# First layer of the edges' net made transposed in four column groups of PE, and one sum moved to GpSimd

## The chip, the cores and the metric

The kernel runs on one core of one Trainium2 chip. The core has engines that each take their own instructions in order: PE (TensorE, matrix products; PEld is its loading of the held operand), DVE (VectorE), ACT (ScalarE), POOL (GpSimd, which here also issues the gathers) and SP (SyncE, which issues plain transfers). The metric is the device time of one execution, in microseconds (us). Before the change it is 2907.54 us, the median of three runs (2907.07 to 2909.65).

## The reference

The layer works on 3125 nodes of 512 values and 50000 edges between them, sorted by the node they end in. It adds a message-passing part and a linear attention to the nodes, then a mixture of eight experts. What the change touches is the message of an edge:

```python
ip1 = jnp.einsum('eum,eum->eu', p1[edge_dst], p1[edge_src]) / 3.0
s0 = jnp.concatenate([pd0, pd0, ip1], axis=-1)
w = ssp(edge_attr @ W_f1) @ W_f2 * (ssp(s0 @ W_s1) @ W_s2)
w1, w2, w3, w4 = jnp.split(w, 4, axis=-1)
out0 = w1 * x0e * sh0[:, None] + w4 * (jnp.einsum('eum,em->eu', x1e, sh1) / jnp.sqrt(3.0))
out1 = w2[:, :, None] * x0e[:, :, None] * sh1[:, None, :] + w3[:, :, None] * x1e * sh0[:, None, None]
out = jax.ops.segment_sum(edge_feat, edge_dst, num_segments=old_x.shape[0])
```

Here `s0` has three blocks of 128 per edge. The first two are values of the end node, so their share of `s0 @ W_s1` (32 values) is made once per node; only `ip1 @ W_s1[256:]` is left for each edge. `x1e . sh1` is a sum of three terms, one for each component.

## The kernel before, in words

All is fp32. A first stage lays the edges out in records sorted by end node, scatters them with GpSimd, makes the nodes' values, and writes two tables of rows to memory: `rows_d` (416 values for the end node, the first 32 of them its share of the first layer) and `rows_s` (896 for the start node). The second stage is the loop over the edges. The third stage runs the experts.

The loop works on tiles of 128 edges, two tiles to a pair (a step `s`), two pairs to a quad `q`. There are 212 pairs always run and some more under a condition on the chip, which does not hold here. The order of PE, ACT, DVE and POOL in it is the order of the code in `run_pairs`, written out by hand: each step runs pieces of several quads and pairs, and `due(n)` says for which quad a piece is due `n` pairs ahead of the pair that is being summed up. The pieces that matter here:

- `fetch` (nine pairs ahead): POOL issues four gathers a step, two of `gd` rows (L710) and two of `gx` rows (L714); SP loads the quad's records `rec` (L699). `gd` has three buffers of a quad, so a new one waits for its last reader three quads before.
- `products` (L726, DVE), `turn` (L734, PE, twelve transposes that also sum the three components of `ip1`) and `turn2` (L743, ACT): `ip`, with features on the partitions.
- `hidden` (four pairs ahead): PE multiplies `ip`, held, with `w_s1c` (L750), for each tile 128 edges by 32; ACT copies the other net's first layer `h1` out of the records (L752).
- `hidden2` (three ahead): DVE adds the end node's share from `gd` (L758). `softplus` on ACT (L763, L766, L769) and `softplus2` on DVE (L774, two ahead) make the shifted softplus.
- `turn_hidden`: PE transposes both first layers, 128 edges by 4 tiles x 32, so that the 32 hidden values of tile `i` lie on partitions 32i to 32i+31 (L779, L780); ACT copies them to `hT` (L785).
- `weigh` (one ahead): PE multiplies 32-row slices of `hT` with the second layers, for two tiles of each net (L801, L805), ACT scales and copies the first (L808, L811), DVE multiplies with the second (L812).
- `dots` (L822, ACT, two ahead) makes the first two terms of `x1 . sh1`; `dots2` (one ahead, DVE) adds them (L830) and adds the third term (L832).
- `which` (L842), `feats` (L860, L867 on ACT, L871, L876): the message. `gather_up` (L884) sums messages into their nodes on PE, `keep_sums` (L893) adds them to the nodes.
- In every sixth step POOL also issues a transfer of an expert's weights (L900).

The PSUM pool `ps_a` has one buffer of each name, `work` has two.

Of the kernel before, what the change touches and what calls it, by code (L numbers as in the profile page):

```python
# [8 lines left out]
F32 = mybir.dt.float32  # L9
I32 = mybir.dt.int32  # L10
AF = mybir.ActivationFunctionType
ALU = mybir.AluOpType
# [4 lines left out]
P = 128  # L17
# [3 lines left out]
G = 4  # L21
REC = 48
USED = 40
CT = 28
HID = 32
# [18 lines left out]
def gnn_mix_moe_kernel(ctx: ExitStack, tc: tile.TileContext, a: dict, out: bass.AP):  # L44
# [5 lines left out]
    nc = tc.nc  # L50
# [25 lines left out]
    ident = const.tile([P, P], F32, name="ident")  # L76
# [46 lines left out]
    with ExitStack() as c1:  # L123
# [313 lines left out]
        work = c1.enter_context(tc.tile_pool(name="work1", bufs=2, reuse_waits="tile"))  # L437
# [42 lines left out]
        for g in range(2):  # L480
            nc.scalar.copy(kx[:, g, :], ps_kx[g])
            ps = psum.tile([P, 4, P], F32, name="ps_kxT", tag="mm")
# [3 lines left out]
            ps = psum.tile([P, GH * HD], F32, name="ps_kv", tag="mm")  # L486
            for k in range(4):
                nc.tensor.matmul(
                    ps, kxT[:, k, g * P : (g + 1) * P], w_v[:, k, g * GH * HD : (g + 1) * GH * HD],
                    start=(k == 0), stop=(k == 3),  # L490
# [4 lines left out]
            ps = psum.tile([P, 2, P], F32, name="ps_kvT", tag="mm")  # L495
# [3 lines left out]
            ps = psum.tile([P, D], F32, name="ps_kvw", tag="mm")  # L499
# [4 lines left out]
            ps = psum.tile([P, 1], F32, name="ps_ks", tag="mm")  # L504
# [4 lines left out]
        for k, w_nd in enumerate((w_nd0, w_nd1)):  # L509
# [4 lines left out]
            ps = psum.tile([P, P], F32, name="ps_ww", tag="mm")  # L514
# [9 lines left out]
        for c in range(NCH):  # L524
            m = cn(c)
            cols = slice(c * CH, c * CH + m)
            for g in range(2):
                ps = psum.tile([P, CH], F32, name="ps_q", tag="mm")
# [5 lines left out]
                ps = psum_b.tile([P, CH], F32, name="ps_nm", tag="mb")  # L534
# [23 lines left out]
        for c in range(NCH):  # L558
            m = cn(c)
            cols = slice(c * CH, c * CH + m)  # L560
            hT = work.tile([P, 2, CH], F32, name="hT", tag="pair")
            for f in range(2):
                ps = psum.tile([P, CH], F32, name="ps_g1", tag="mm")
# [5 lines left out]
            for f in range(2):  # L569
                ps = psum.tile([P, CH], F32, name="ps_g2", tag="mm")  # L570
# [11 lines left out]
            ps = psum.tile([P, CH], F32, name="ps_p0", tag="mm")  # L582
# [3 lines left out]
            for t in tiles_of(c):  # L586
# [6 lines left out]
                ps = psum.tile([P, HID + 3 * MUL], F32, name="ps_p1", tag="mm")  # L593
                nc.tensor.matmul(ps[:n, :HID], p0[:, lo : lo + n], w_s1p, start=True, stop=True)
                for b in range(3):
                    nc.tensor.matmul(
                        ps[:n, HID + b * P : HID + (b + 1) * P], xT[:, 1 + b, t * P : t * P + n], w_pre1,
                        start=True, stop=True,
                    )
                nc.scalar.copy(r[:n, : HID + 3 * MUL], ps[:n])  # L600
                ps = psum.tile([P, D], F32, name="ps_nd", tag="mm")
                for b in range(4):
                    nc.tensor.matmul(
                        ps[:n, b * P : (b + 1) * P], xg[:, b, lo : lo + n], w_nd0 if b == 0 else w_nd1,
                        start=True, stop=True,
# [8 lines left out]
                ps = psum_b.tile([P, D], F32, name="ps_own", tag="mb")  # L614
# [4 lines left out]
                for b in range(4):  # L619
                    last = nc.tensor.matmul(  # L620
                        ps[:n, b * P : (b + 1) * P], xg[:, b, lo : lo + n], w_ndo[0 if b == 0 else 1],
                        start=False, stop=(b == 3),
# [43 lines left out]
    with ExitStack() as c2:  # L666
        w = c2.enter_context(tc.tile_pool(name="w2", bufs=1, reuse_waits="tile"))
        gat = c2.enter_context(tc.tile_pool(name="gat", bufs=4, reuse_waits="tile"))
        work = c2.enter_context(tc.tile_pool(name="work2", bufs=2, reuse_waits="tile"))
        ps_a = c2.enter_context(tc.tile_pool(name="ps_a", bufs=1, space=PSUM, reuse_waits="tile"))  # L670
# [3 lines left out]
        w_s1c = w.tile([P, HID], F32, name="w_s1c")  # L674
# [17 lines left out]
        quads = [Quad() for _ in range(NQ)]  # L692

        def fetch(q, k):

            Q = quads[q]
            if k == 0:
                Q.rec = gat.tile([P, G, REC], F32, name="rec2", bufs=6)
                loaded = nc.sync.dma_start(  # L699
                    Q.rec, recs[q * G * P : (q + 1) * G * P, :].rearrange("(p i) f -> p i f", i=G)  # L700
                )
# [3 lines left out]

                Q.gd = gat.tile([P, G, HID + 3 * MUL], F32, name="gd", bufs=3)
                Q.gx = gat.tile([P, G, 3 * MUL + D], F32, name="gx", bufs=5)
            reci = Q.rec.bitcast(I32)
            for i in (2 * k, 2 * k + 1):
# [33 lines left out]
            nc.scalar.copy(Q.ip, Q.ps_ip)  # L743

        def hidden(q):
            Q = quads[q]
            Q.ps = ps_a.tile([P, 3, P], F32, name="ps_h")
            ps = Q.ps[:, 2, :].rearrange("p (i f) -> p i f", f=HID)
            for i in range(G):
                nc.tensor.matmul(ps[:, i, :], Q.ip[:, i, :], w_s1c, start=True, stop=True)  # L750
            Q.h1 = work.tile([P, G, HID], F32, name="h1")
            nc.scalar.copy(Q.h1, Q.rec[:, :, 8:USED])  # L752

        def hidden2(q):
            Q = quads[q]
            Q.h = work.tile([P, G, HID], F32, name="h2")
            ps = Q.ps[:, 2, :].rearrange("p (i f) -> p i f", f=HID)
            nc.vector.tensor_add(Q.h, ps, Q.gd[:, :, :HID])  # L758

        def softplus(q):  # L760
            Q = quads[q]
            sp = work.tile([P, G, HID], F32, name="sp")
            nc.scalar.activation(sp, Q.h, AF.Abs)  # L763
            if q * PR < NPR_MOST:
                with tc.issue_after(table.ins):
                    nc.scalar.activation(sp, sp, AF.Exp, scale=-1.0)  # L766
            else:
                nc.scalar.activation(sp, sp, AF.Exp, scale=-1.0)
            nc.scalar.activation(sp, sp, AF.Ln, bias=half, scale=0.5)  # L769
            Q.sp = sp  # L770

        def softplus2(q):
            Q = quads[q]
            nc.vector.scalar_tensor_tensor(Q.h, Q.h, 0.0, Q.sp, op0=ALU.max, op1=ALU.add)  # L774

        def turn_hidden(q):

            Q = quads[q]
            nc.tensor.transpose(Q.ps[:, 0, :], Q.h1.rearrange("p i f -> p (i f)"), ident)  # L779
            nc.tensor.transpose(Q.ps[:, 1, :], Q.h.rearrange("p i f -> p (i f)"), ident)  # L780

        def turn_hidden2(q):
            Q = quads[q]
            Q.hT = work.tile([P, 2, P], F32, name="hT")
            nc.scalar.copy(Q.hT, Q.ps[:, :2, :])  # L785

        pairs = [Quad() for _ in range(NPR)]

        def parts(s):

            return quads[s // 2], (s % 2 * 2, s % 2 * 2 + 1)
# [22 lines left out]
        def dots(s):  # L814

            Q, tiles = parts(s)
            R = pairs[s]
            R.dot = work.tile([P, 2, PR, MUL], F32, name="dot")
            x = Q.gx[:, :, 3 * MUL :]
            for c in (1, 2):  # L820
                for k, i in enumerate(tiles):
                    nc.scalar.activation(  # L822
                        R.dot[:, c - 1, k, :], x[:, i, c * MUL : (c + 1) * MUL], AF.Copy, scale=Q.rec[:, i, c : c + 1]
                    )

        def dots2(s):
            Q, tiles = parts(s)
            R = pairs[s]
            x = Q.gx[:, :, 3 * MUL :]
            nc.vector.tensor_add(R.dot[:, 0], R.dot[:, 0], R.dot[:, 1])  # L830
            for k, i in enumerate(tiles):
                nc.vector.scalar_tensor_tensor(  # L832
                    R.dot[:, 0, k, :], x[:, i, 3 * MUL :], Q.rec[:, i, 3:4], R.dot[:, 0, k, :],
                    op0=ALU.mult, op1=ALU.add,
                )
# [69 lines left out]
        def run_pairs(lo, hi):  # L905

            with tc.manual_schedule(
                engines={
                    mybir.EngineType.PE, mybir.EngineType.Activation, mybir.EngineType.DVE, mybir.EngineType.Pool
                }  # L910
            ):
                LEAD = 9
                for s in range(lo - LEAD, hi):
                    def due(ahead):

                        q, r = divmod(s + ahead, PR)
                        return [q] if r == 0 and lo <= q * PR < hi else []

                    if s + LEAD < hi:
                        fetch((s + LEAD) // PR, (s + LEAD) % PR)  # L920
                    if s >= lo and s % 6 == 0 and mats:
                        line_up(*mats.pop(0))
                    for q in due(3):
                        hidden2(q)
                    for q in due(2):
                        softplus2(q)
                    if lo <= s + 1 < hi:
                        which(s + 1)
                        dots2(s + 1)
                    for k in range(2):  # L930
                        for q in due(7 - k):
                            products(q, k)
                    if lo <= s - 1:
                        keep_sums(s - 1)
                    if lo <= s + 1 < hi:
                        weigh(s + 1)
                    for q in due(2):
                        turn_hidden(q)
                        turn_hidden2(q)
                    for q in due(3):  # L940
                        softplus(q)
                    for q in due(5):
                        turn(q)
                    if lo <= s + 2 < hi:
                        dots(s + 2)
                    if lo <= s + 1 < hi:
                        feats(s + 1)
                    for q in due(5):
                        turn2(q)
                    if lo <= s:  # L950
                        gather_up(s)
                    for q in due(4):
                        hidden(q)
                keep_sums(hi - 1)


        run_pairs(0, NPR_MOST)
        while mats:
            line_up(*mats.pop(0))
# [10 lines left out]
    with ExitStack() as c3:  # L970
# [17 lines left out]
        with tc.tile_pool(name="work3", bufs=2) as work:  # L988
# [165 lines left out]
            for k in range(2):  # L1154
                for t0 in range(0, NT, 5):
# [16 lines left out]
                    for i in range(5):  # L1172
                        nc.tensor.matmul(
                            ps_i, los[:, i, :], what[:, i, :, :],
                            start=(k == 0 and t0 + i == 0), stop=(k == 1 and t0 + i == NT - 1),
# [229 lines left out]
```

## Time and profile before

| what | value |
|---|---|
| median of three runs | 2907.54 us |
| the profiled execution | 2907.43 us, span 2905.7 us, granted clock 0.942 |
| PE, DVE, ACT, POOL busy in the whole span | 2508.4, 1865.2, 1463.4, 1762.2 us |
| the same between 1000 and 1500 us (the loop) | 487.0, 494.3, 423.6, 344.8 us |
| DMA share and rate there | 0.81, 259 GB/s |

The profile is one execution. Busy times are of instructions on an engine; the ends of matrix products are modelled, so a busy PE need not be at its peak. The loop over the edges runs from about 720 us to about 1985 us. In the views of instructions in order of time, a bracket says how long the engine had been idle and what released it ("issue" is nothing that the profile shows).

### The profile page before, as it was taken

The numbers are of one execution on the slowest core, as the hardware profiler recorded it, in microseconds if no ns is written. First come the engines' busy times: TensorE is split into PE (matmuls) and PEld (weight loads), VectorE is DVE, ScalarE is ACT, GpSimd is POOL, SyncE is SP. The second block draws the span as 40 slices with busy tenths as digits, with TensorE's granted clock in tenths as the row PEclk, the third lists the DMA queues.
The fourth block names the chain that finished last, engine by engine and source line by source line (L and its number), as shares of the span: only waits on it lengthen the run. The fifth ranks groups of instructions, "written<-read, shape, count | busy, mean of one in ns | idle before, by whom it ended". The sixth has DMA issues, their size and how long they took to land. (4 is left out here: it accounts for less than half of the span.)

```text
span 2905.7 us, 41979 instructions
## 1 busy us (share of the span) xinstructions
PE 2508.4 (86%) x13530; PEld 1631.8 (56%) x13530; DVE 1865.2 (64%) x3864; ACT 1463.4 (50%) x4183; POOL 1762.2 (61%) x1756
## 2 busy tenths in 40 slices
PE   2685999005999999999999999997499999999998
PEld 2463466003444444444444444444388888888887
DVE  5887322005999999999999999996722222222222
ACT  2472422003888888888888888884311111111111
POOL 1777766677766666666666666750255555555553
PEclk8897999556999999999999999999799999999999
DMA  6662066107888888888888887853642622975452
GB/s 261 205 221 86 27 234 217 44 27 236 268 258 258 259 257 258 255 262 257 258 258 257 259 258 251 256 181 116 252 150 72 226 87 71 323 276 200 168 189 98
DMA packets 191644, 588.10 MB, mean 202 GB/s; under 512 B 54405, under 2 KB 79418, under 8 KB 179384
## 3 DMA queue, kind: packets, MB, share of 16 engines
q0 software_dynamic: 135216, 496.50, 52.4%
q1 hardware_dynamic: 49864, 82.54, 8.5%
q10 hardware_dynamic: 6336, 6.28, 0.7%
q8 instruction: 111, 1.82, 0.2%
q14 instruction: 117, 0.96, 0.1%
HBM read 635.54 MB, written 119.53 MB: 260 GB/s over the span
## 5 line engine op out<-in xcount | busy, mean ns | idle before, releaser
L884 PE MATMUL ps_s<-ft,one 128*128 128x512 f32 x1696 | 765.3, 594 | 2.1 <-DVE ft L871 2.0
L710 POOL DMA_INDIRECT gd<-rows_d,rec x424 | 429.7, 1013 | 266.0 <-DVE h L758 158.2
L714 POOL DMA_INDIRECT gx<-rows_s,rec x424 | 434.9, 1026 | 129.2 <-issue 123.4
L395 POOL DMA_INDIRECT recs<-again,at_i x392 | 413.7, 1055 | 156.2 <-issue 122.1
L867 ACT ACTIVATE ft<-ft,rec 128x128 f32<-128x128 f32 x1272 | 395.3, 389 | 193.8 <-DVE ft L860 193.7
L884 PEld LDWEIGHTS ps_s<-ft,one 128*128 128x128 f32 x1696 | 312.2, 194 | 310.7 <-issue 231.2
L1280 ACT ACTIVATE h<-ps_f,bias 128x128 f32<-128x128 f32 x318 | 116.7, 367 | 620.8 <-PE ps_f L1267 617.0
L1267 PE MATMUL ps_f<-h,we 128*128 128x128 f32 x3392 | 401.3, 277 | 0.0
L1282 DVE TENSOR_SCALAR h<-ps_f,bias 128x128 f32<-128x128 f32 x318 | 111.4, 351 | 433.4 <-PE ps_f L1267 429.4
L1267 PEld LDWEIGHTS ps_f<-h,we 128*128 128x128 f32 x3392 | 386.9, 192 | 1.4
L1194 POOL DMA_INDIRECT we<-w_rows,w_at x212 | 215.1, 1014 | 222.2 <-PE ps_y L1298 98.0
L734 PE MATMUL ps_ip<-ident,prod 128*128 128x128 f32 x1272 | 165.9, 281 | 172.1 <-DVE prod L726 172.1
L734 PEld LDWEIGHTS ps_ip<-ident,prod 128*128 128x128 f32 x1272 | 140.3, 143 | 252.1 <-issue 249.3
L822 ACT ACTIVATE dot<-gx,rec 128x128 f32<-128x128 f32 x848 | 270.6, 397 | 0.0
L812 DVE TENSOR_TENSOR wt<-wt,wb 128x1024 f32<-128x1024 f32 x212 | 257.7, 1216 | 0.0
L805 PE MATMUL wb<-w_s,hT 32*128 32x512 f32 x848 | 240.8, 644 | 2.9 <-DVE wt L812 2.9
L801 PE MATMUL wa<-w_f,hT 32*128 32x512 f32 x848 | 240.0, 642 | 0.0
L726 DVE TENSOR_TENSOR prod<-gd,gx 128x768 f32<-128x768 f32 x212 | 201.9, 952 | 23.1 <-DMA gx<-rows_s,rec 23.1
L1267 PEld LDWEIGHTS ps_f<-xt,we 128*128 128x128 f32 x1696 | 199.4, 193 | 26.0 <-issue 23.4
L871 DVE TENSOR_TENSOR ft<-gx,wt 128x768 f32<-128x768 f32 x212 | 205.7, 970 | 0.0
L1267 PE MATMUL ps_f<-xt,we 128*128 128x128 f32 x1696 | 199.8, 277 | 0.7 <-ACT xt L1215 0.7
L1298 PE MATMUL ps_y<-we,h 128*128 128x512 f32 x424 | 196.1, 605 | 0.0
(303 smaller groups left out, 3755.6 us busy)
## 6 DMA issues: line engine op xcount, KB each, us to landing
w_rows<-in_Wh POOLq DMA_DIRECT2D x24, 1024.0 KB
rows_s<-r SPq DMA_DIRECT2D x24, 448.0 KB
recs<-zero POOLq DMA_DIRECT2D x10, 1056.0 KB
rec<-recs SPq DMA_DIRECT2D x106, 96.0 KB
lined<-rec SPq DMA_DIRECT2D x14, 672.0 KB
again<-lined POOLq DMA_DIRECT2D x14, 672.0 KB
w_rows<-in_Wo POOLq DMA_DIRECT2D x8, 1024.0 KB
gd<-rows_d,rec POOLq DMA_INDIRECT x424
```

The source lines that it names most:

```text
L395: put = nc.gpsimd.indirect_dma_start(out=recs[:, :], out_offset=bass.IndirectOffsetOnAxis(ap=at_i[:, t : t + 1], axis=0), in_=again[c][:, ...
L710: nc.gpsimd.indirect_dma_start(out=Q.gd[:, (i + 2) % G, :], out_offset=None, in_=rows_d[:, :], in_offset=bass.IndirectOffsetOnAxis(ap=reci ...
L714: Q.last = nc.gpsimd.indirect_dma_start(out=Q.gx[:, i, :], out_offset=None, in_=rows_s[:, :], in_offset=bass.IndirectOffsetOnAxis(ap=reci[ ...
L734: nc.tensor.matmul(ps[:, i, :], Q.prod[:, i, b * P : (b + 1) * P], ident, is_transpose=True, start=(b == 0), stop=(b == 2),)
L801: nc.tensor.matmul(wa[:, k, :], Q.hT[r, 0, :], w_f2[r, :], start=True, stop=True)
L805: nc.tensor.matmul(wb[:, k, :], Q.hT[r, 1, :], w_s2[r, :], start=True, stop=True)
L812: nc.vector.tensor_mul(R.wt, R.wt, wb)
L822: nc.scalar.activation(R.dot[:, c - 1, k, :], x[:, i, c * MUL : (c + 1) * MUL], AF.Copy, scale=Q.rec[:, i, c : c + 1])
L867: nc.scalar.activation(R.ft[:, k, D + c * MUL : D + (c + 1) * MUL], R.ft[:, k, 2 * D :], AF.Copy, scale=Q.rec[:, i, c : c + 1],)
L884: nc.tensor.matmul(R.ps, R.one[:, k, :], R.ft[:, k, m * D : (m + 1) * D], start=(k == 0 and m == 0), stop=(k == 1 and m == 1),)
L1194: nc.gpsimd.indirect_dma_start(out=dst, out_offset=None, in_=src, in_offset=bass.IndirectOffsetOnAxis(ap=at[:, j : j + 1], axis=0), bounds ...
L1267: nc.tensor.matmul(pss[f], ws[l][:, k, f * P : (f + 1) * P], h[:, k, :], start=(k == 0), stop=(k == 3))
```

## The change

`hidden` now makes both first layers transposed at once. For tile `i` the 32 columns of the records, the 32 columns of `gd` and the weights `w_s1c` are held in columns 32i to 32i+31 of PE; the identity (twice) and `ip` are streamed; the second and third go to the same place in PSUM, which adds them. With that L750's old form, the copy L752, the sum L758, the transposes L779 and L780 and the copy L785 go. `softplus` reads PSUM and copies the first net's half to `hT`, `softplus2` reads PSUM and writes the second half. The sum of the first two terms of `x1 . sh1` goes from DVE (in `dots2`) to GpSimd (in `dots`, one step earlier in the code).

```diff
         def hidden(q):
             Q = quads[q]
-            Q.ps = ps_a.tile([P, 3, P], F32, name="ps_h")
-            ps = Q.ps[:, 2, :].rearrange("p (i f) -> p i f", f=HID)
+            Q.ps = ps_a.tile([P, 2, P], F32, name="ps_h")
             for i in range(G):
-                nc.tensor.matmul(ps[:, i, :], Q.ip[:, i, :], w_s1c, start=True, stop=True)
-            Q.h1 = work.tile([P, G, HID], F32, name="h1")
-            nc.scalar.copy(Q.h1, Q.rec[:, :, 8:USED])
-
-        def hidden2(q):
-            Q = quads[q]
-            Q.h = work.tile([P, G, HID], F32, name="h2")
-            ps = Q.ps[:, 2, :].rearrange("p (i f) -> p i f", f=HID)
-            nc.vector.tensor_add(Q.h, ps, Q.gd[:, :, :HID])
+                nc.tensor.matmul(
+                    Q.ps[i * HID : (i + 1) * HID, 0, :], Q.rec[:, i, 8:USED], ident,
+                    start=True, stop=True, tile_position=(0, i * HID),
+                )
+            for i in range(G):
+                nc.tensor.matmul(
+                    Q.ps[i * HID : (i + 1) * HID, 1, :], Q.gd[:, i, :HID], ident,
+                    start=True, stop=False, tile_position=(0, i * HID),
+                )
+            for i in range(G):
+                nc.tensor.matmul(
+                    Q.ps[i * HID : (i + 1) * HID, 1, :], w_s1c, Q.ip[:, i, :], start=False, stop=True,
+                    tile_position=(0, i * HID),
+                )
...
-            sp = work.tile([P, G, HID], F32, name="sp")
-            nc.scalar.activation(sp, Q.h, AF.Abs)
+            sp = work.tile([P, P], F32, name="sp")
+            nc.scalar.activation(sp, Q.ps[:, 1, :], AF.Abs)
...
             Q.sp = sp
+            Q.hT = work.tile([P, 2, P], F32, name="hT")
+            nc.scalar.copy(Q.hT[:, 0, :], Q.ps[:, 0, :])
...
-            nc.vector.scalar_tensor_tensor(Q.h, Q.h, 0.0, Q.sp, op0=ALU.max, op1=ALU.add)
-
-        def turn_hidden(q):
-
-            Q = quads[q]
-            nc.tensor.transpose(Q.ps[:, 0, :], Q.h1.rearrange("p i f -> p (i f)"), ident)
-            nc.tensor.transpose(Q.ps[:, 1, :], Q.h.rearrange("p i f -> p (i f)"), ident)
-
-        def turn_hidden2(q):
-            Q = quads[q]
-            Q.hT = work.tile([P, 2, P], F32, name="hT")
-            nc.scalar.copy(Q.hT, Q.ps[:, :2, :])
+            nc.vector.scalar_tensor_tensor(
+                Q.hT[:, 1, :], Q.ps[:, 1, :], 0.0, Q.sp, op0=ALU.max, op1=ALU.add
+            )
...
+            nc.gpsimd.tensor_add(R.dot[:, 0], R.dot[:, 0], R.dot[:, 1])
 
         def dots2(s):
             Q, tiles = parts(s)
             R = pairs[s]
             x = Q.gx[:, :, 3 * MUL :]
-            nc.vector.tensor_add(R.dot[:, 0], R.dot[:, 0], R.dot[:, 1])
...
-                    for q in due(3):
-                        hidden2(q)
...
-                    for q in due(2):
-                        turn_hidden(q)
-                        turn_hidden2(q)
```

## The prediction

> **What bounds the kernel now.** I read the page's busy table and slices first, then the busy time by stage, the instructions of one stretch of the edge loop in order of time on each engine, and last the list of who waited for whom.
>
> The page: engine, busy us (share) x instructions; then busy tenths in 40 slices of 72.6 us.
>
> ```profile
> PE 2508.4 (86%) x13530; PEld 1631.8 (56%) x13530; DVE 1865.2 (64%) x3864; ACT 1463.4 (50%) x4183; POOL 1762.2 (61%) x1756
> ...
> PE   2685999005999999999999999997499999999998
> ...
> DVE  5887322005999999999999999996722222222222
> ...
> POOL 1777766677766666666666666750255555555553
> ```
>
> Slices 11 to 27 are the edge loop. There PE and DVE both stand at 9, so shares cannot say which sets the pace. The stage row (start:end, length, busy time of PE, PEld, DVE, ACT, POOL, clock, DMA share, GB/s) is closer:
>
> ```profile
> 1000.00:1500.00 500.00, 487.01 (x2216) 247.03 (x2217) 494.31 (x905) 423.63 (x1316) 344.83 (x343) 1.00 0.81 259
> ```
>
> DVE is without work for 6 us in 500. The order of time settles it. Columns: start, length, engine, line, operation, tiles, [idle before <- who ended it].
>
> ```profile
> 1424.94 0.70 PE L801 MATMUL wa<-w_f,hT 32*128 32x512 f32 x2
> ...
> 1426.02 0.33 PE L779 MATMUL ps_h<-ident,h 128*128 128x128 f32 x1
> 1426.65 0.33 PE L780 MATMUL ps_h<-ident,h 128*128 128x128 f32 x1 [0.30 <-DVE h L774]
> 1426.81 3.60 PE L884 MATMUL ps_s<-ft,one 128*128 128x512 f32 x8
> 1430.25 0.97 PE L750 MATMUL ps_h<-w_s1c,ip 128*128 128x32 f32 x8
> 1431.15 0.70 PE L801 MATMUL wa<-w_f,hT 32*128 32x512 f32 x2
> ...
> 1432.22 1.53 PE L734 MATMUL ps_ip<-ident,prod 128*128 128x128 f32 x12
> 1433.59 3.60 PE L884 MATMUL ps_s<-ft,one 128*128 128x512 f32 x8
> 1437.12 0.70 PE L801 MATMUL wa<-w_f,hT 32*128 32x512 f32 x2
> ```
>
> One quad (two pairs) takes 1437.12 - 1424.94 = 12.18 us; the loop has 106. PE's one real hole in it is the wait for DVE at L780. DVE itself:
>
> ```profile
> 1407.66 0.42 DVE L876 TENSOR_TENSOR ft<-wt,dot 128x256 f32<-128x256 f32 x1
> 1408.00 0.29 DVE L758 TENSOR_TENSOR h<-ps_h,gd 128x128 f32<-128x128 f32 x1
> 1408.20 0.42 DVE L842 TENSOR_TENSOR one<-lane,rec 128x256 f32<-128x256 f32 x1
> 1408.53 0.42 DVE L830 TENSOR_TENSOR dot<-dot 128x256 f32<-128x256 f32 x1
> 1408.99 0.62 DVE L832 SCALAR_TENSOR_TENSOR dot<-gx,rec,dot 128x128 f32<-128x128 f32 x2
> ```
>
> Each starts as the one before ends, and no bracket names a wait: DVE paces the loop, PE follows closely. POOL, which only issues transfers here, is third:
>
> ```profile
> 1420.73 1.22 POOL L710 DMA_INDIRECT gd<-rows_d,rec  x1 [1.94 <-DVE h L758]
> ...
> 1430.02 0.95 POOL L714 DMA_INDIRECT gx<-rows_s,rec  x1 [0.30 <-issue]
> 1432.91 1.22 POOL L710 DMA_INDIRECT gd<-rows_d,rec  x1 [1.94 <-DVE h L758]
> ```
>
> It waits once a quad until L758 has read `gd`.
>
> **The change, part by part, for one quad of 12.18 us.** Costs are from start to next start, since neighbours overlap by some 0.1 us.
>
> *DVE.* L758 goes: 1408.00 to 1408.20, 0.20. L830 goes twice: 1408.53 to 1408.99, 0.46 each. L774 now reads PSUM in place of one SBUF operand; L758, of the same 128x128 with a PSUM operand, takes 285 ns against L774's 322, so I count nothing. DVE needs 12.18 - 0.20 - 0.92 = 11.06.
>
> *ACT.* L752 (282 ns) goes; L785 (384 ns, 256 wide) becomes a copy of 128, some 0.28 by L752. That is 0.4 less on an engine with 10.3 busy per 12.18 (423.63 of 500): off the path, worth nothing by itself.
>
> *PE.* Gone are the two transposes with their hole (1426.02 to 1426.81, 0.79) and L750 (1430.25 to 1431.15, 0.90): 12.18 becomes 10.49. New are twelve products with 32 columns held and 128 streamed. Fp32 products that are not transposes go as two instructions (L750 shows x8 for four), so 24. One with 128 streamed costs 0.107 by L884 (3.44 us for eight of 512, a quarter of 0.43) and 0.114 by L734 (1.37 for twelve). Bounds: one after another, 24 x 0.114 = 2.74, PE 13.23; four column groups at a time, 6 x 0.114 = 0.68 and some 0.2 to enter, PE 11.4. The 0.2 is from L801/L805: four 32-row products, two instructions of 0.43 each, end within 1.08 us and not in 3.4, so four parts of the array do work side by side. That is rows, not columns, but it is the nearest row, so I take 11.4. The hole at L780 has no successor: L774 is followed by L801/L805 a whole step later.
>
> "TensorE: Matmul & The Clock Gate", Part 3, has three column tiles reach 2.38 times the speed of one. No run here shows it; by that figure the group is an estimated 2.74/2.38 = 1.15 and PE 11.6, by the rows above 11.4, and neither is the bound.
>
> *POOL.* The quad's eight issues run from 1420.73 to 1430.97, 10.24, and the next needs 0.30 to start. L900 adds 0.80 in one quad of three (0.27). POOL needs 10.81 and so has 1.37 to spare. Into each step the change puts an add of 128x256, behind the four gathers of that step (and L900) and ahead of the four of the next. It waits for ACT's two L822 pairs of the step, which lie well before the end of the four issues once POOL is the late one. Behind it wait the gathers, which have nine pairs of lead, and DVE's L832 one step later. The gather of `gd` is now released by PE's products of the step before (near 1431.1 in the stretch shown) and no longer by L758.
>
> No row shows an add on POOL. Nearest rows on it:
>
> ```profile
> L101 POOL IOTA pair_no_i<- 128x220 int32 x1 | 0.3, 301 | 0.0
> L101 POOL IOTA each_i<- 128x56 int32 x1 | 0.2, 164 | 0.0
> ```
>
> 137 ns for 164 elements is 0.84 ns each and 0.12 fixed. With 256 elements, one pass costs 0.33, two passes (one per operand read) 0.55, three (the result too) 0.76. I take 0.66. DVE's own 0.42 lies inside. What it loses beside a full DVE no row shows either: nothing at the low end, one DVE operation (0.95, L726) at the high end. POOL's present issues have a median of 0.946 and a mean of 1.013 for L710, 0.07 lost; DVE will mostly be waiting for this very add, so I take 0.10, near the low end. Two adds are 1.52 and POOL needs 12.33.
>
> "SBUF — State Buffer", section "Who interferes with whom", speaks against the move: a VectorE instruction with two SBUF inputs and a GpSimd instruction that reads SBUF exclude each other for a whole instruction. No row here shows it. "GPSIMD Engine Reference" (section 3) has 4497 ns for an add of 2048, an estimated 0.56 for 256: by that alone POOL needs 11.93 and the kernel gains some 26 us; by the exclusion it loses up to a DVE operation more each time.
>
> *DMA.* The same bytes; at a share of 0.81 it has room.
>
> *Sum.* Bound before: DVE 12.18. After: POOL 12.33, PE 11.4, DVE 11.06. So +0.15 x 106 = +16 us. The profiled execution took 2907.43 (span 2905.7), the median is 2907.54; outside the loop nothing changes. 2907.4 + 16 = 2923. DVE's gain of 1.12 a quad turns into waiting for POOL at L832.
>
> **The rivals.**
>
> A, faster: the adds are cheap, one pass (0.33), or run inside the 0.30 gaps ahead of the issues. POOL needs 11.47, PE 11.4, DVE 11.06; with 0.1 for imperfect overlap 11.57, -0.61 x 106 = -65, 2843. For it: each gap is marked "issue", not work. Against: an add has two inputs. The point that decides is (12.18 - 10.81)/2 = 0.685 per add all told; anything below gains, at 0.55 some 29 us (2878).
>
> B, slower, collision: each add costs its 0.66 and half a DVE operation or more (1.1). POOL needs 13.0, +0.83 x 106 = +88, 2995. For it: DVE stays busy 11.06 of 12.33. Against: POOL paces, so DVE is idle when the add runs.
>
> C, slower, the column groups do not overlap: PE 13.23, +1.05 x 106 = +111, 3018. For it: 0.43 per instruction at L884 shows no overlap between whole-array products. Against: L801/L805.
>
> D, the parts do nothing because something else holds 12.18, such as the chain ACT L811, DVE L812 and L860, ACT L867, ACT L808: 0.57 + 1.25 + 0.61 + 1.87 + 0.83 is about 5.1 a pair, under 6.09. It does not hold.
>
> **How the numbers follow.** Forecast (adds of 0.69 to 0.9 all told, 2909 to 2953) 0.31; B 0.15, C 0.15; A with all adds under 0.685: 0.39, of which a quarter near its end. About 0.2% (5.8 us, 0.055 a quad) is what a measurement of this kernel can tell from no change; adds of 0.66 to 0.71 fall there, 0.08: 0.03 of A and 0.05 of the forecast. Faster 0.36, same 0.08, slower 0.56. The forecast's own range is 2909 to 2953. Cases of both signs hold most of the chance, so the range reaches from A's end, 2845 (0.1 below), to near C's, 3010 (0.1 above).
>
> **What would show it.** After: some 3546 DVE instructions (106 + 212 fewer), 1968 on POOL, 15014 on PE, 4077 on ACT. Right: POOL in the loop near 10 tenths with no wait for DVE at L710, DVE with holes before the STTs of the dots released by POOL, adds of 0.6 to 0.8, the 24 small products within about 0.9 us. Wrong: adds under 0.6 or the gap ahead of the next issue gone (A); DVE operations of twice their length beside the adds (B); the small products spread over 2.5 us and PE without holes (C).

## The result and the profile after

The changed kernel takes 3046.95 us (median of 4 runs, 3035.73 to 3052.56) against 2908.60 for the kernel before beside it (4 runs, 2907.07 to 2910.47): 1.0471 times as long, with a 95% interval of 1.0445 to 1.0498. The forecast was +16 us and a range up to 3010; measured are +138. The sign was right, and the size was outside the range. The profiled execution took 3052.56 us with a span of 3050.8.

The page of the kernel after: the busy table, then busy tenths in 40 slices of 76.3 us.

```profile
PE 2625.3 (86%) x15014; PEld 1624.8 (53%) x15014; DVE 1843.0 (60%) x3546; ACT 1427.3 (47%) x4077; POOL 2067.6 (68%) x1968
...
DVE  5886322016888888888888888888642222222222
...
POOL 1777666668888888888888888883145555555552
```

The counts of DVE, ACT, POOL and PE are those forecast. DVE has fallen from 9 to 8 tenths in the loop, and POOL has risen from 6 to 8. It does not show 9, because the gaps of 0.3 us ahead of its issues are not counted as busy. The stage row (start:end, length, busy time of PE, PEld, DVE, ACT, POOL, clock, DMA share, GB/s) has 437.6 of 500 for DVE, where it had 494.3:

```profile
1000.00:1500.00 500.00, 481.74 (x2514) 219.60 (x2514) 437.60 (x704) 369.49 (x1148) 419.67 (x384) 0.99 0.77 235
```

The groups of instructions of POOL in the loop, from 1000 to 1900 us (count | busy us, mean ns of one | idle before, and what ended it), and the one group of DVE that grew:

```profile
L714 POOL DMA_INDIRECT gx<-rows_s,rec x267 | 343.5, 1287 | 81.4 <-issue 80.5 <-ACT dot L820 0.9
L710 POOL DMA_INDIRECT gd<-rows_d,rec x267 | 268.8, 1007 | 61.7 <-issue 61.7
L823 POOL TENSOR_TENSOR dot<-dot 128x256 f32<-128x256 f32 x133 | 127.7, 960 | 1.9
...
L840 DVE TENSOR_TENSOR one<-lane,rec 128x256 f32<-128x256 f32 x133 | 104.8, 788 | 0.0
```

133 adds in 900 us make 6.77 us a pair (13.5 a quad, where it was 12.18), and POOL is taken for all of it: 4.59 for four issues (343.5 + 268.8 over 133.5), 1.07 for the gaps ahead of them, 0.96 for the add, 0.14 for the weights. So POOL paces the loop, as forecast. Two of these rows are longer than they should be. L714 was 1018 ns before and is 1287 now, on the same transfers. L840, which the change does not touch, was 414 ns (L842 there) and is 788. PE's share of 481.74 in 500 does not say that PE paces: the first experiment below has the same PE instructions and goes at 11.93 us a quad.

The list of waits of the kernel after (engine, tile and line that waits <- who ends it: us in total, times, longest) has the hole that was forecast for DVE:

```profile
DVE dot L830 <- POOL dot L823: 107.2, 133, 1.7
```

The order of time shows where POOL's time goes (start, length, engine, line, operation, tiles, [idle before <- who ended it]); three products of DVE are shown beside it. L869 and L840 read both inputs from SBUF; L810 has one of its two in PSUM:

```profile
1400.45 0.95 DVE L869 TENSOR_TENSOR ft<-gx,wt 128x768 f32<-128x768 f32 x1
1400.59 1.63 POOL L714 DMA_INDIRECT gx<-rows_s,rec  x1 [0.30 <-issue]
...
1401.85 0.79 DVE L840 TENSOR_TENSOR one<-lane,rec 128x256 f32<-128x256 f32 x1
...
1402.24 0.97 POOL L823 TENSOR_TENSOR dot<-dot 128x256 f32<-128x256 f32 x1
...
1403.25 0.61 DVE L830 SCALAR_TENSOR_TENSOR dot<-gx,rec,dot 128x128 f32<-128x128 f32 x2 [0.61 <-POOL dot L823]
1403.37 1.06 POOL L710 DMA_INDIRECT gd<-rows_d,rec  x1 [0.16 <-issue]
...
1404.74 0.95 POOL L714 DMA_INDIRECT gx<-rows_s,rec  x1 [0.30 <-issue]
...
1405.25 1.21 DVE L810 TENSOR_TENSOR wt<-wt,wb 128x1024 f32<-128x1024 f32 x1
...
1406.00 0.95 POOL L710 DMA_INDIRECT gd<-rows_d,rec  x1 [0.30 <-issue]
...
1407.10 0.95 DVE L869 TENSOR_TENSOR ft<-gx,wt 128x768 f32<-128x768 f32 x1
1407.26 1.62 POOL L714 DMA_INDIRECT gx<-rows_s,rec  x1 [0.31 <-issue]
```

Three of four issues of this step take 0.95 to 1.06. The last one begins 0.14 to 0.16 us after DVE's 768-wide product L869, and takes 1.62. Then the add meets L840, and both are long. The rows in order of time from 1000 to 1900 us show the same throughout. All 133 issues that start while L869 runs take 1.58 to 1.65. All 134 that start while L810 runs, which is longer than L869, take 0.94 to 0.95. And 110 of the 133 adds start 0.37 to 0.60 us behind L840, with medians of 0.98 for the add and 0.79 for L840; the other 23 stand behind an issue of the experts' weights, meet no product and take 0.86 to 0.87.

### The profile page after: what moved, and what is told of

Same layout as the page of the kernel before. It is cut to its first block, busy times and chain, and to the rows that moved or that the text cites. A ratio compares the mean times of both kernels' runs of the same rounds, so it can differ in the third digit from the quotient of the medians.

```text
span 3050.8 us, 45674 instructions
## 1 busy us (share of the span) xinstructions
PE 2625.3 (86%) x15014; PEld 1624.8 (53%) x15014; DVE 1843.0 (60%) x3546; ACT 1427.3 (47%) x4077; POOL 2067.6 (68%) x1968
## 5 line engine op out<-in xcount | busy, mean ns | idle before, releaser
L882 PE MATMUL ps_s<-ft,one 128*128 128x512 f32 x1696 | 785.1, 606 | 48.6 <-DVE ft L869 48.1
L714 POOL DMA_INDIRECT gx<-rows_s,rec x424 | 541.1, 1276 | 129.2 <-issue 128.0
L810 DVE TENSOR_TENSOR wt<-wt,wb 128x1024 f32<-128x1024 f32 x212 | 257.7, 1216 | 1.3 <-ACT wt L809 1.3
L830 DVE SCALAR_TENSOR_TENSOR dot<-gx,rec,dot 128x128 f32<-128x128 f32 x424 | 130.2, 349 | 167.7 <-POOL dot L823 167.7
L823 POOL TENSOR_TENSOR dot<-dot 128x256 f32<-128x256 f32 x212 | 203.5, 960 | 33.8 <-DVE wt L810 17.1
L726 DVE TENSOR_TENSOR prod<-gd,gx 128x768 f32<-128x768 f32 x212 | 201.9, 952 | 19.8 <-DMA gx<-rows_s,rec 19.8
L869 DVE TENSOR_TENSOR ft<-gx,wt 128x768 f32<-128x768 f32 x212 | 202.8, 957 | 0.0
```

What stands on the lines that cost most here:

```text
L714: Q.last = nc.gpsimd.indirect_dma_start(out=Q.gx[:, i, :], out_offset=None, in_=rows_s[:, :], in_offset=bass.IndirectOffsetOnAxis(ap=reci[ ...
L810: nc.vector.tensor_mul(R.wt, R.wt, wb)
L882: nc.tensor.matmul(R.ps, R.one[:, k, :], R.ft[:, k, m * D : (m + 1) * D], start=(k == 0 and m == 0), stop=(k == 1 and m == 1),)
```

## The experiments

Times from different chips are compared by their ratio to the kernel before on the same chip; between the first five experiments and the result plain differences are given too, since the kernel before took 2908 to 2911 us beside each of them. The letters in the expectations are theories, each named where it first stands. The one that lasted is R: an instruction of POOL that reads SBUF (the add, but also the issue of a gather, which by the code takes its row numbers from `rec`) and an instruction of DVE with two inputs in SBUF exclude each other. By R the one that starts to read first holds the other up (DVE's records overlap their neighbours by some 0.1 us, so a product may read a little later than its line says). The runs show the exclusion. The rule of order covers most meetings and not all: L840 started first above and was long as well, which R does not explain.

**The column groups alone** (the sum back on DVE, in `dots2`):

```diff
-            nc.gpsimd.tensor_add(R.dot[:, 0], R.dot[:, 0], R.dot[:, 1])   # in dots
+            nc.vector.tensor_add(R.dot[:, 0], R.dot[:, 0], R.dot[:, 1])   # in dots2
```

> The column groups alone, the sum back on DVE. Theory P (POOL's add sets the pace of the changed kernel): POOL has room again, DVE paces with 11.06 + 0.92 = 11.98 a quad, 0.20 less than before, so about 2886. Rival G (the column groups cost the time): it stays above 3000. Rival E (DVE and POOL exclude each other only through the add): same as P here.

Measured: 2882.78 us (2877.91 to 2890.04, 4 runs) against 2908.35; ratio 0.9912, interval 0.9880 to 0.9944. The column groups gain 25 us, and the whole loss comes with the sum on POOL. The stage row has DVE full again, and from the second line to the third PE takes one quad of 11.93 us (forecast from the removed L758 alone: 12.18 - 0.20 = 11.98):

```profile
1000.00:1500.00 500.00, 483.69 (x2848) 224.55 (x2847) 494.19 (x880) 418.05 (x1299) 358.28 (x350) 1.00 0.82 264
```

```profile
1403.02 0.70 PE L799 MATMUL wa<-w_f,hT 32*128 32x512 f32 x2
...
1414.95 0.70 PE L799 MATMUL wa<-w_f,hT 32*128 32x512 f32 x2
```

It is also the fastest version of this study.

**The sum on POOL alone** (the kernel before, with the same line moved the other way):

```diff
+            nc.gpsimd.tensor_add(R.dot[:, 0], R.dot[:, 0], R.dot[:, 1])   # in dots
-            nc.vector.tensor_add(R.dot[:, 0], R.dot[:, 0], R.dot[:, 1])   # in dots2
```

> GpSimd's sum alone, the first layer as before. Theory P: POOL takes 6.75 a pair as in the changed kernel, perhaps a little more because L710 waits again for DVE's read of gd: 3047 to 3080. Rival G: at or below 2907, since DVE loses 0.92 a quad.

Measured: 2964.01 us (2957.62 to 2984.28, 5 runs); ratio 1.0185, interval 1.0157 to 1.0213. It is slower, but only by 56 us, and so the expected size was missed. The same add on the same queue costs less here. The groups from 1000 to 1900 us and two steps in order of time show another partner for it:

```profile
L825 POOL TENSOR_TENSOR dot<-dot 128x256 f32<-128x256 f32 x141 | 107.0, 759 | 2.0
...
L876 DVE TENSOR_TENSOR ft<-wt,dot 128x256 f32<-128x256 f32 x141 | 147.2, 1044 | 0.0
```

```profile
1403.20 1.08 DVE L876 TENSOR_TENSOR ft<-wt,dot 128x256 f32<-128x256 f32 x1
1403.25 0.74 POOL L825 TENSOR_TENSOR dot<-dot 128x256 f32<-128x256 f32 x1
...
1405.27 0.94 DVE L726 TENSOR_TENSOR prod<-gd,gx 128x768 f32<-128x768 f32 x1
1405.42 1.62 POOL L714 DMA_INDIRECT gx<-rows_s,rec  x1 [0.31 <-DVE dot L832]
```

The add keeps its own 0.74 us. What is held up is DVE's L876, which takes 1044 ns in place of 415. DVE then shows 497 of 500 busy, which is partly waiting in disguise. The long issue is now the second of a step, beside L726, and no longer the one ahead of the add; 71 of 567 issues take more than 1.3 us here, against 133 of 534 in the kernel after. The theory that tied the long issue to its place ahead of POOL's own operation (K) falls here: the issue is long beside whichever 768-wide product it starts behind.

**A write in place of the add** (the kernel after, but the first two terms are not summed; POOL clears an unused tile of the same size):

```diff
-            nc.gpsimd.tensor_add(R.dot[:, 0], R.dot[:, 0], R.dot[:, 1])
+            R.junk = work.tile([P, PR, MUL], F32, name="junk")
+            nc.gpsimd.memset(R.junk, 0.0)
```

> The sum of the first two terms is left out; POOL fills an unused tile of the same 128x256 with zeros instead, so it reads nothing. Theory K (a compute instruction lengthens the issue ahead of it, whatever it reads): the fourth issue of a step stays at 1.62, the fill is 0.2 to 0.35, POOL takes 5.0 + 0.13 + 0.68 + 0.3 = 6.1 a pair, about 2910. Theory E (the reads of POOL and DVE exclude each other and that lengthens both the add and the issue): the issue falls to 0.95, L840 is 0.42 throughout, POOL no longer paces and the kernel is at DVE's 11.06 or PE's 11.3 a quad, about 2815.

Measured: 2902.37 us (one run). The issue did not stay long in K's place, and the time is far above the other expectation of 2815. The groups (1000 to 1900 us) and one step:

```profile
L710 POOL DMA_INDIRECT gd<-rows_d,rec x297 | 344.7, 1160 | 69.6 <-issue 62.4 <-DMA gd<-rows_d,rec 2.0 <-PE ps_s L883 1.5
L714 POOL DMA_INDIRECT gx<-rows_s,rec x297 | 330.7, 1113 | 90.5 <-issue 68.8 <-ACT ft L866 6.4 <-DMA gd<-rows_d,rec 4.9
L824 POOL MEMSET junk<- 128x256 f32 x148 | 51.9, 351 | 0.0
...
L841 DVE TENSOR_TENSOR one<-lane,rec 128x256 f32<-128x256 f32 x148 | 62.3, 421 | 1.5 <-PE ps_s L883 1.4
```

```profile
1405.22 0.95 DVE L870 TENSOR_TENSOR ft<-gx,wt 128x768 f32<-128x768 f32 x1
1405.40 1.59 POOL L714 DMA_INDIRECT gx<-rows_s,rec  x1 [0.30 <-issue]
```

With the add gone, DVE's 256-wide product is back at its 0.42; the clearing never runs beside it in these 900 us. It does run beside L726 in 38 steps, and L726 keeps its 0.94 to 0.96. The issues are not back at 0.95: their means are 1160 and 1113 ns, and 148 steps in 900 us make 6.08 a pair, with POOL still fully taken. So even an operation of 0.35 gains next to nothing. In the kernel before, POOL stood still once a quad until L758 had released it, and its issues had means of 1019 and 1018; 8 of 591 took more than 1.3 us. Here 144 of 594 do, all but one of them beside L870 or L726. My reading is that the wait for L758 set POOL back in step with DVE each time, and that a POOL with no time to spare starts its issues beside the 768-wide products more often. No run tests this by itself.

**The add between the second and the third issue** (the kernel after; `fetch` is called twice a step, for one tile each, the second time after `dots`):

```diff
-                        fetch((s + LEAD) // PR, (s + LEAD) % PR)
+                        fetch((s + LEAD) // PR, (s + LEAD) % PR, 0)   # issues of tile 2k
...
+                    if s + LEAD < hi:                                  # behind dots
+                        fetch((s + LEAD) // PR, (s + LEAD) % PR, 1)   # issues of tile 2k + 1
```

> The add stands between the second and the third issue of a step instead of after the fourth; the same work. Theory K: the second issue becomes 1.62 and the fourth 0.95, the time stays within 15 us of 3047. Rival F (the fourth issue is long for its own sake, by what it gathers or by where it falls in DVE's step): the fourth stays at 1.62 and the second at 0.95.

Measured: 2979.62 us (one run). Neither expectation held. The same instructions in another order shifted the meetings, and in this stretch the long issue is the one that starts behind L726:

```profile
1408.34 0.95 DVE L726 TENSOR_TENSOR prod<-gd,gx 128x768 f32<-128x768 f32 x1
...
1408.70 1.42 POOL L714 DMA_INDIRECT gx<-rows_s,rec  x1 [0.30 <-issue]
```

L726 ends there at 1409.29. The issue ends 0.83 us after it (1410.12), as in the kernel after: L869 ends at 1401.40, and the issue beside it at 1402.22, 0.82 later.

**DVE's product L840 behind the dots** (the kernel after, two calls exchanged):

```diff
-                        which(s + 1)
                         dots2(s + 1)
+                        which(s + 1)
```

> DVE's comparison of lane and place (L840) stands behind the dots (L830) instead of ahead of them; the same work. Theory R (a POOL instruction that reads SBUF, the add as much as the issue of a gather with its list of places, and a DVE instruction with two SBUF inputs exclude each other, and who started first holds the other up to its end): the add of 0.98 met L840 under way; now DVE waits idle for it, so the add falls to 0.74 to 0.86, L840 is 0.42 throughout, POOL 6.53 a pair instead of 6.75, -0.22 x 212 = -47, about 3000. Rival Q (the add simply takes 0.96 on POOL): the add and the time stay, 3047 within 10.

Measured: 2959.27 us (2953.29 to 2961.53, 4 runs); ratio 1.0178, interval 1.0157 to 1.0199. The direction was right and the gain was larger than expected, 88 us against 47, since the last issue became short as well as the add. Rival Q (the add takes 0.96 on POOL whatever stands beside it) falls. Groups from 1000 to 1900 us, then one step:

```profile
L823 POOL TENSOR_TENSOR dot<-dot 128x256 f32<-128x256 f32 x143 | 108.6, 759 | 2.1
...
L874 DVE TENSOR_TENSOR ft<-wt,dot 128x256 f32<-128x256 f32 x143 | 151.0, 1056 | 0.0
L840 DVE TENSOR_TENSOR one<-lane,rec 128x256 f32<-128x256 f32 x143 | 59.0, 413 | 0.0
```

```profile
1408.44 1.00 DVE L869 TENSOR_TENSOR ft<-gx,wt 128x768 f32<-128x768 f32 x1
1408.45 0.95 POOL L714 DMA_INDIRECT gx<-rows_s,rec  x1 [0.30 <-issue]
1409.37 1.08 DVE L874 TENSOR_TENSOR ft<-wt,dot 128x256 f32<-128x256 f32 x1
1409.42 0.73 POOL L823 TENSOR_TENSOR dot<-dot 128x256 f32<-128x256 f32 x1
...
1411.43 0.95 DVE L726 TENSOR_TENSOR prod<-gd,gx 128x768 f32<-128x768 f32 x1
1411.58 1.61 POOL L714 DMA_INDIRECT gx<-rows_s,rec  x1 [0.30 <-DVE one L840]
```

L840 is back at 413 ns, and the add at 759, as R has it. But the add now meets L874, which pays 1056 in place of 419. The last issue starts within 0.01 us of L869 and takes 0.95. The loss has moved and become smaller. No instruction was added or taken away, and yet the time changed by 3%: where the meetings fall is a large part of the price.

One thing here goes beyond R as it is worded. In 23 of the 24 steps with an issue of the experts' weights (L898, a plain transfer without row numbers), that issue starts 0.02 to 0.04 us behind L874, and L874 takes 0.95. So an issue seems able to hold up a product without fetching row numbers, and which of its accesses matters is not shown.

**One SBUF input less in DVE's 768-wide product.** In the kernel after, L869 multiplies with the hidden layers in PSUM, in place of the third weights:

```diff
+            quads[0].late = Q.ps
...
-                w3.unsqueeze(2).to_broadcast([P, PR, 3, MUL]),
+                quads[0].late[:, 0:1, :].unsqueeze(1).to_broadcast([P, PR, 3, MUL]),
```

> L869 multiplies with the hidden layers in PSUM instead of w3, so the third weights are left out of the result; its size is the same, but it has one SBUF input instead of two. Theory R: the last issue of a step, 1.62 because it starts 0.14 behind L869, falls to 0.95 there, POOL takes at most 6.75 - 0.68 = 6.07 a pair and with other meetings up to 6.4: 2903 to 2975. Rival S (the last issue is long for its own sake, by its place or by the transfers under way): it stays at 1.62 and the time at 3047.

Measured: 2948.09 us (2944.21 to 2952.86, 4 runs); ratio 1.0139, interval 1.0115 to 1.0162. The issue beside this product (L870 in this kernel) is no longer long, which was the point of the run:

```profile
1403.79 0.95 DVE L870 TENSOR_TENSOR ft<-gx,ps_h 128x768 f32<-128x768 f32 x1
...
1403.97 0.95 POOL L714 DMA_INDIRECT gx<-rows_s,rec  x1 [0.30 <-issue]
```

From 1000 to 1900 us, 25 issues start 0.1 to 0.2 us behind L870 and take 0.94 to 0.95; 45 start as far behind L726, which still has both inputs in SBUF, and take 1.61 to 1.65. The control has the same edit without the sum on POOL:

> Control for the run before: the same PSUM operand in L869 with the sum on DVE as in the run with the column groups alone; the third weights are left out of the result. DVE paces there, L869's length does not change, so 2883 within 15 by both theories; under R the issues that met L869 are short, which frees POOL and gives nothing.

Measured: 2949.24 us (one run), a miss: 2883 was expected. The edit has a price of its own. PE may not overwrite the hidden layers before DVE has read them, as the control's list of waits shows:

```profile
PE ps_h L751 <- DVE ft L870: 70.2, 71, 1.0
```

Both runs carry this new wait, so their times do not measure R. The lengths of their instructions do.

**The same with a constant in PSUM.** To get rid of that wait, the operand became 128 values in a third of the same PSUM tile, written once:

```diff
+        ps_all = ps_a.tile([P, 3, P], F32, name="ps_h")
+        ps_c3 = ps_all[:, 2, :]
+        nc.vector.memset(ps_c3, 0.5)
...
-            Q.ps = ps_a.tile([P, 2, P], F32, name="ps_h")
+            Q.ps = ps_all[:, :2, :]
...
-                w3.unsqueeze(2).to_broadcast([P, PR, 3, MUL]),
+                ps_c3.unsqueeze(1).unsqueeze(1).to_broadcast([P, PR, 3, MUL]),
```

> The kernel after, but the 768-wide product of the features on DVE (the kernel after's L869) multiplies with a constant that lies in PSUM (128 values in the unused third of the PSUM tile ps_h, written once) in place of the weights w3 in SBUF: the third weights are left out, the two SBUF inputs become one, and PE has nothing to wait for in that tile, unlike in the run with the hidden layers as the operand. R (a POOL instruction that reads SBUF and a DVE instruction with two SBUF inputs exclude each other): POOL's last issue takes 0.95 us in place of 1.62 wherever it stands beside this product; 6.75 us a pair less 0.67 gives 6.08, or 2905; later issues that now slip behind the products L726 (0.95 long) can take back up to half of it, so 2890 to 2975. S (the issue's length has nothing to do with the operands of the DVE instruction beside it): 1.62 stays and the time is 3047 within 15.

> The control of that: the column groups alone, the sum on DVE, and the same constant in PSUM as the operand of the 768-wide product. R and S: there is no POOL instruction but the issues; DVE paced this version without the constant (2883), and the product keeps its 0.95, so 2883 within 15 if the edit has no price of its own. If it has one, as the edit with the hidden layers had (2949), the difference to 2883 is that price and has to be taken off before the times of the pair are compared.

Measured, on a chip where the kernel before took 3053.86 us beside them: 3078.63 (ratio 1.0064, interval 1.0034 to 1.0095) with the sum on POOL, and 3400.28 (1.1124, 1.1089 to 1.1158) without. Both expected times were missed. The wait did not go; PE still waits for the product (72 times in 900 us with the sum, 57 without). With the sum:

```profile
PE ps_h L753 <- DVE ft L872: 75.3, 72, 2.5
```

Without the sum PE's wait is longer, 177.5 us in 900 against 75.3, but why is not settled; nothing is drawn from these two times. But the run with the sum has the cleanest pair of lines of the study, in one kernel and within 16 us:

```profile
1408.37 0.95 DVE L872 TENSOR_TENSOR ft<-gx,ps_h 128x768 f32<-128x768 f32 x1
1408.56 0.95 POOL L717 DMA_INDIRECT gx<-rows_s,rec  x1 [0.31 <-issue]
...
1423.67 0.94 DVE L729 TENSOR_TENSOR prod<-gd,gx 128x768 f32<-128x768 f32 x1
1423.83 1.62 POOL L717 DMA_INDIRECT gx<-rows_s,rec  x1 [0.30 <-issue]
```

Both products are 768 wide and take 0.95. The same issue starts 0.19 us after the one and 0.16 after the other. Beside the product with an operand in PSUM it takes 0.95; beside the product with two inputs in SBUF it takes 1.62. It is so for all of them from 1000 to 1900 us: 23 issues start 0.1 to 0.2 us behind L872 and take 0.94 to 0.95, 40 as far behind L729 and take 1.61 to 1.62. So the exclusion of R is shown on the issue of a gather, and its rival, that the operands have nothing to do with it, falls.

## Why the prediction was wrong in size

- **Counts, PE, DVE.** The counts are as forecast. DVE's 437.6 of 500 are 11.85 a quad of 13.5; without the 0.75 by which two L840 are longer that is 11.1, against 11.06 forecast. PE's 11.4 as a bound was not met by any run; the version with the column groups alone shows only that it is at most 11.93. The 24 small products of the column groups run four at a time: they begin at 1405.08 and the next product of PE at 1405.88, 0.80 us against 0.88 forecast (lines below). Rival C (2.74) falls. L758's 0.20 is confirmed by the version with the column groups alone.

```profile
1405.08 0.42 PE L750 MATMUL ps_h<-ident,rec 128*32 128x128 f32 x8
...
1405.54 0.40 PE L760 MATMUL ps_h<-ip,w_s1c 128*32 128x128 f32 x8
1405.88 1.13 PE L799 MATMUL wa<-w_f,hT 32*128 32x512 f32 x4
```

- **The add's own length.** Forecast 0.66 from the IOTA rows; measured 0.73 to 0.75 where it keeps its own length. This is 0.08 of a miss in each pair, 17 us in 212 pairs.
- **What the add loses beside DVE: the step that failed first.** "DVE will mostly be waiting for this very add, so I take 0.10, near the low end." DVE does wait for the add, but only at L830. When the add starts, DVE is still at L840, one instruction earlier (1401.85 against 1402.24). The add has a mean of 0.96 in place of 0.66 + 0.10 = 0.76: 0.20 a pair, 42 us (this includes the 17).
- **What the issues lose: the step that cost most, a term that the sum put at nothing.** POOL's 10.81 a quad was taken over from the kernel before: 5.27 a pair for four issues with their gaps. After, they take 4.59 + 1.07 = 5.66: 0.39 a pair, 83 us. The 10.81 looked like a constant of POOL, but it was a length beside DVE's instructions as they then lay, where 8 of 591 issues took more than 1.3 us; after, 133 of 534 did. Together 0.59 x 212 = 125 us, and 2923 + 125 = 3048 against 3047 measured. This only accounts for the miss with measured lengths; nobody forecast it.
- **Rival B** had the mechanism (each add collides with DVE), a sum of 2995, and an argument against it that was wrong: "POOL paces, so DVE is idle when the add runs". Its sign, DVE operations of twice their length beside the adds, is what L840 shows. Its sum was too low as well, since it counted only the adds and not the issues.
- **Rival A** (a cheap add gains 65 us) would have failed even with a cheap add. With an operation of 0.35 us on POOL the time is 2902, only 6 us below the kernel before, in one run. By the undisturbed lengths (0.74 + 4 x 0.95 + 1.07 + 0.14 = 5.75 a pair, 11.5 a quad) POOL would have had room below 12.18. That is an estimate, and no run here shows such a kernel.
- **The rule that was weighed and set aside.** The Trainium skill's page "SBUF — State Buffer", section "Who interferes with whom", was drawn on in the prediction as speaking against the move, with "No row here shows it". The runs show it: beside the add L874 and L876 take 1.07 to 1.10 in place of 0.42, and the add and L840 are both long. The rows of the kernel before had shown it too, for the issues: the prediction gave their median 0.946 and mean 1.013, and did not ask beside which instructions the 0.07 was lost. One of them, in the list of the kernel before, is 1.17 long beside L726:

```profile
1409.52 0.95 DVE L726 TENSOR_TENSOR prod<-gd,gx 128x768 f32<-128x768 f32 x1
...
1410.12 1.17 POOL L714 DMA_INDIRECT gx<-rows_s,rec  x1 [0.31 <-issue]
```

It began at 1410.12 and L726 ended at 1410.47. The issue ended at 1411.29, 0.82 later: the same distance as above.

## What to carry to other kernels

Before moving work to GpSimd, look at what its present instructions lose: put those that are longer than their median beside the VectorE instructions that run at their start. If these have two inputs in SBUF, the engine's room is not what its busy time says, and the order of the two engines' instructions is a price of its own (88 us here for exchanging two calls). And cost a change with two parts as two: here one gained 25 us by itself, and the other lost 56 by itself and 164 beside the first.

## What the runs showed of the hardware

- The issue of an indirect gather by GpSimd, 0.95 us by itself, takes 1.62 where it starts 0.14 to 0.16 us behind a 768-wide VectorE product with two inputs in SBUF, and 0.95 where it starts 0.18 to 0.19 us behind a product of the same length with one input in PSUM. It ends 0.81 to 0.84 us after the product, in all the long ones shown here. That an issue is held up by a VectorE product, I had not expected.
- How the two meet decides who pays. The add of 128x256 on GpSimd keeps its 0.74 us where VectorE's 256-wide product begins 0.04 to 0.07 us ahead of it, and the product then takes 1.07 to 1.10 us in place of 0.42 (116 times in the run with the sum on POOL alone). Where the product is 0.37 to 0.60 us ahead, both are long (0.98 and 0.79 at the median, 110 times in the kernel after). Why the earlier one is long too is open.
- Clearing 128x256 on GpSimd takes 0.35 us and leaves the 768-wide product L726 beside it at 0.94 to 0.96, though that has both inputs in SBUF.
